# Cross attention by single key tiles in two score banks, maxima in the other two, running sums on GpSimd, attention output through DRAM

## The chip, the cores and the metric

The kernel runs on one core of a Trainium2 chip. The time is that of the device in microseconds, as the median of several runs; before the change it is 4902.3 us (three runs, 4899.26 to 4904.04).

## What is computed

A gated block on x of shape (8, 1024, 512) with a context of shape (8, 1024, 384), all in float32:

```python
x = x + tanh(g_xattn) * cross(layernorm(x), ctx)
x = x + tanh(g_ffn) * selfattn(layernorm(x))
# cross: 8 heads of 64; q = x Wq, k = ctx Wk, v = ctx Wv
#   softmax(q k^T / 8) v, then Wo and a bias
# selfattn: 16 heads of 32; q is normalized per head, shifted and scaled;
#   softmax(q k^T / sqrt(32)) v = h; a gate per token from softmax(h Wr) (best 3 of 15)
#   and softmax(h Ws); out = (h * gate) Wp + bias
```

Both attentions are full softmaxes over 1024 keys; the kernel subtracts a row maximum before each exponential.

## The kernel before

**Phases and chunks.** There are 16 phases: for each of the 8 batch elements one cross phase (kind 1) and one self phase (kind 2), in the order cross 0, cross 1, self 0, cross 2, self 1 and so on. A phase has four chunks of 128 channels, which are two heads of width 64 in a cross phase and four heads of width 32 in a self phase. A chunk goes through steps (`Chunk.steps`): for each half h of 512 queries, over the key tiles of 128. In a self phase a step is one key tile, so 16 steps a chunk; in a cross phase it is two key tiles (`nk` = 2), so 8 steps.

**A step.** `score` (line 677) multiplies k by q with the array cut into row groups of 32 or 64 ("rows" here), into two pairs of PSUM banks of the pool `ps_sc`, each pair one tile of 128 x 1024. At the first step of a half the negated row maxima (`sh`) are put in by a product with ones; later steps add the product with the difference of key tiles (`differences`, line 547), so the shift stays in the bank, and the scores of a step can be written only when the exponentials of the step before have been read. ScalarE takes the exponentials of each pair (line 723). `value` (line 824) multiplies them with v, with the array cut into column groups of 32 or 64 ("columns"), into one bank that is kept over a half. The sums of the exponentials: `paired` (line 728) adds two exponential tiles on GpSimd, `add` (line 735) adds such a result to the running one on VectorE if that is free and not `behind`, or else keeps it apart, and `summed` (line 756) multiplies what is left with ones on TensorE. A cross step pairs its own two tiles, a self step pairs with the next step. At the end of a half, ScalarE copies the values into `hT`, a tile in SBUF for each half, and `multiplied` (line 818) divides by the sum on GpSimd. `hT` has one buffer for each half, so a new phase may write it only when the output projection of the phase before has read it; `value` runs projections until that is so.

**Maxima.** For each coming chunk, all scores are computed once more beforehand in bfloat16 (`scores`, line 589) and reduced on VectorE. `unit` (line 600) does this for one head, 128 queries and 512 keys, in one of the three banks of `ps_gen`; a chunk has 32 (cross) or 64 (self) of them. `row_epoch` (line 913) puts some beside the scores of a step, `visit` (line 1010) does some between two column products, which changes the cutting of the array twice. When they are complete, `turn` transposes them and sends them to `sh` by DMA.

**Fills.** Between the steps lie the projections of other chunks and phases, the "fills", as two streams: `projector` (q and k of coming chunks) and `others` (output projection of the phase before, gates, and v of the next phase). They use the three banks of `ps_gen` too.

**What sets the order.** Each engine's order is fixed when the program is built. The builder keeps a clock for each engine (`clock`) with costs written by hand (`MM` 862 ns for a column product, `CHANGE` for a change of the array's cutting, `on("DVE", 690)` and so on), and decides by it. `attend` (line 958) goes through a chunk: scores of the next step, values of this one, then fills up to a quota from `COSTS`, and `until` waits, fills or visits until the scores' banks come free. `wanted` (line 975) gives the rate of maxima per step over three coming chunks, and `credit` adds it up.

Of the kernel before, what the change touches and what calls it, by code (L numbers as in the profile page):

```python
# [16 lines left out]
P = 128  # L17
# [4 lines left out]
def tile_gated_block(  # L22
# [62 lines left out]
    ps_sc = ctx.enter_context(tc.tile_pool(name="ps_sc", bufs=2, space=bass.MemoryType.PSUM))  # L85
# [106 lines left out]
    CHANGE = {(32, 128): 105, (64, 128): 105, (128, 32): 105, (128, 64): 110, (128, 128): 110}  # L192
    LOADED, LANDED, RATE = 3500, 5500, 0.0008
    COSTS = {1: (54, 28, 30, 30), 2: (50, 20, 22, 26)}
# [9 lines left out]
    deferred = []  # L204

# [77 lines left out]
    class Stream:  # L283

        def __init__(self, g):
            self.g = g
            self.step()
# [10 lines left out]
    def work(flow):  # L298

        ready = [(not s.mid, n) for n, s in enumerate(flow) if s.ready() <= now() + 20]  # L300
        if ready:
            s = flow[min(ready)[1]]
        else:
            s = min(flow, key=lambda s: s.ready())
            if s.ready() == NEVER:
                return False
        s.step()
        if not s.ready:
            flow.remove(s)
        flush()  # L310
        return True
# [101 lines left out]
    class Chunk:  # L413


        def __init__(self, kind, b, c):
# [4 lines left out]
            self.nk = 4 // self.nh  # L421
            self.ns = NT // self.nk
# [124 lines left out]
        def differences(self):  # L547

            w, n = self.nk * P, self.ns // 2
# [59 lines left out]

        def fours(self):  # L610
# [3 lines left out]
            for u in range(2):  # L614
# [13 lines left out]
            tiles = [  # L628
                ps_sc.tile([P, 2, H], F32, tag="sc", name=f"pm_{self.key}_{self.left}_{u}")
                for u in range(2)  # L630
            ]
# [45 lines left out]
        def score(self, step, order):  # L677
# [3 lines left out]
            if s == 0:  # L681
                self.pss = {}
                for u in order:
                    slot, free = least(places)
                    tile_u = ps_sc.tile([P, 2, H], F32, tag="sc", name=f"sc_{key}_{h}_{u}")
                    self.pss[u] = [tile_u, slot, free]
                    places[slot] = free

            def products(m, u):
                done = 0.0  # L690
                for j in (2 * u, 2 * u + 1):
                    kk, i = divmod(j, nh)
                    r, kc = i * width, s * self.nk + kk
# [5 lines left out]
                    else:  # L699
                        part = slice(r, r + width)  # L700
                        array((width, P))
                        lhsT, rhs = self.k[part, ts(kc, P)], self.q[part, ts(h, H)]
# [3 lines left out]
                        tile_u[:, j % 2, :],  # L706
# [9 lines left out]
            for half in [order] if self.kind == 1 else [order[:1], order[1:]]:  # L716
                for m in range(1 if s else 0, 2):
                    for u in half:
                        done[u] = products(m, u)
            e = {}  # L720
            for u in order:
                e[u] = Exps(f"e_{key}_{h}_{s}_{u}")
                nc.scalar.activation(e[u].tile, self.pss[u][0], AF.Exp)  # L723
                e[u].ready = on("ACT", 975, done[u], e[u].free)
                self.pss[u][2] = places[self.pss[u][1]] = e[u].ready
# [9 lines left out]
        def add(self, h, s, u, a, last):  # L735

            accs = self.acc.setdefault((h, u), [])
            wanted = not behind[0]
            free = clock["DVE"] <= now() + 500
            end = s + 1 >= self.ns  # L740
            if accs and not forced[0] and not (wanted and free) and not (end and now() > a.ready + 1500):
                later.insert(0, (now() + 200, self.add, h, s, u, a, last))
                return
            elif accs and wanted and (free or not end):
                nc.vector.tensor_tensor(accs[-1].tile, accs[-1].tile, a.tile, ALU.add)  # L745
                accs[-1].ready = on("DVE", 1820, accs[-1].ready, a.ready)
                a.used(accs[-1].ready)
                live[0] -= 1
                ready = accs[-1].ready
# [6 lines left out]
        def summed(self, h, end):  # L756

            accs = [self.acc.pop((h, u)) for u in range(self.nh // 2)]
# [59 lines left out]
        def multiplied(self, h, r, ready):  # L818
            hT = self.st.hT[h][:, self.c, :]
            engine = nc.vector if self.ends else nc.gpsimd  # L820
            engine.tensor_tensor(hT, hT, r, ALU.mult)  # L821
            self.st.hT_ready[h][self.c] = on("DVE" if self.ends else "POOL", 1270, ready)

        def value(self, step):

            h, s = step
            width, st = self.width, self.st
            if s == 0:
# [3 lines left out]
            for kk in range(self.nk):  # L832
                kc = s * self.nk + kk
                for i in range(self.nh):
                    j = kk * self.nh + i
                    nc.tensor.matmul(  # L836
                        self.av[ts(i, width), :],
                        lhsT=st.v[:, kc, ts(self.c * self.nh + i, width)],
                        rhs=e[j // 2].tile[:, j % 2, :],
                        start=(kc == 0),  # L840
                        stop=(kc == NT - 1),
                    )
                used = [e[kk]] if self.kind == 1 else [e[0], e[1]]
                done = pe(MM, av_free[0], *(x.ready for x in used))
                for x in used:
                    x.used(done)
                if kk == 0 and self.kind == 1:
                    room(1, self, h)
                    self.paired(h, s, 0, e[0], e[1], True)
                    array((P, width))  # L850
            if self.kind == 2 and s + 2 == self.ns and self.ends:
                for u in range(2):
                    self.whole[h, u] = [e[u], self.e[h, s + 1][u]]
                live[0] += 4
                later.append((now() + 3000, self.summed, h, True))
            elif self.kind == 2 and s % 2 == 0:
                room(2, self, h)
                for u in range(2):
                    self.paired(h, s + 1, u, e[u], self.e[h, s + 1][u], u == 1)
            if s == self.ns - 1:  # L860
                while st.before and st.before.hT_left[h]:
                    assert work(at_work)
                nc.scalar.copy(st.hT[h][:, self.c, :], self.av)
                av_free[0] = on("ACT", 590, done)
                self.divided(h, av_free[0])
            if s % 2 or self.kind == 1:
# [3 lines left out]
        def begun(self):  # L870
            self.whole = {}
            self.e, self.acc, self.parts, self.halves = {}, {}, {}, {}
# [23 lines left out]
    def room(n, ch, h):  # L896

        while live[0] > 5 - n:
# [14 lines left out]
    def row_epoch(ch, step, target, need, kept):  # L913
# [3 lines left out]
        order = (0, 1)  # L917
        at = now() + CHANGE.get(tiling[0], 0) + 30
        ok = target and target.pend and target.left and target.open <= at
        if ok and target.kind == 2 and ch.kind == 2:  # L920
            n = free_banks(at) - kept
# [4 lines left out]
            picks = [i for i in (2 * late, 2 * late + 1) if target.pend[i]]  # L926
            for i in picks[: max(n, 0)]:
                target.unit(i)
            order = (1 - late, late)
        elif ok and target.kind == 1 and free_banks(at) >= 2:  # L930
            for i in range(2):
                if target.pend[i]:
                    target.unit(i)
        ch.score(step, order)
        if not target or target.kind != ch.kind:
            return
        if ch.kind == 2:
            at = min(rows)
            if ok and target.left:
                n = max(free_banks(at + 30) - kept, 0)  # L940
                picks = [i for i in (2 * order[0], 2 * order[0] + 1) if target.pend[i]]
                for i in picks[:n]:
                    target.unit(i)
        elif need > 2 and target.left and target.open <= now() and free_banks(now()) - kept >= 2:
            for i in range(2):
                if target.pend[i]:
                    target.unit(i)

    at_work, at_side, debt = [], [], [0.0]
# [8 lines left out]
    def attend(ch, queue, first, cost):  # L958
# [3 lines left out]
        debt[0] = min(debt[0], 6 * MM) + cost * MM  # L962
        filled, owed = 0.0, debt[0]
        n = len(ch.steps)
        weight = 2 if ch.kind == 1 else 1
        after = queue[0] if queue else None
        credit, last = 0.0, now()

        def target():
            for t in queue[:3]:  # L970
# [4 lines left out]
        def wanted(m):  # L975

            slots, left, rate = (n - m) * weight - 4, 0, 0.0
            for t in queue[:3]:
                left += t.left if t.pend is not None else t.nh * NT * NH
                rate = max(rate, left / max(slots, 1))  # L980
                slots += len(t.steps) * (2 if t.kind == 1 else 1)
            return rate * weight
# [6 lines left out]
        def fill():  # L989
# [5 lines left out]
            debt[0] -= now() - was  # L995
# [14 lines left out]
        def visit(slack=300, least=2, keep=True):  # L1010
# [5 lines left out]
            n = free_banks(at) - (kept() if keep else 0)  # L1016
            some = sorted((i for i in range(t.nh) if t.pend[i]), key=lambda i: -len(t.pend[i]))
            if n < min(least, len(some)):
                return False
            for i in some[:n]:  # L1020
                t.unit(i)
                credit -= 1
            return True

        def until(at, urgent=False):
            while now() < at:
# [5 lines left out]
                if (urgent or credit >= 2) and visit():  # L1032
# [4 lines left out]
        def rows_of(chunk, step):  # L1037
            nonlocal credit
            t = target()
            if t and t.kind != chunk.kind and credit >= 2:  # L1040
                visit(600, keep=False)
            was = t.left if t else 0
            row_epoch(chunk, step, t, credit, 0)
            credit -= was - (t.left if t else 0)
# [5 lines left out]
        for m, step in enumerate(ch.steps):  # L1050
            need = wanted(m)
# [493 lines left out]
```

## Time and profile before

| | |
|---|---|
| profiled execution | 4899.77 us |
| its span, first to last instruction | 4897.9 us |
| clock granted to TensorE, mean | 0.983 |
| TensorE busy | 4792.1 us, 98% |
| VectorE busy | 2728.5 us, 56% |
| ScalarE busy | 2294.7 us, 47% |
| GpSimd busy | 2628.1 us, 54% |
| single maxima on VectorE (line 606) | 3042, mean 684 ns |
| pair adds on GpSimd (line 730) | 764, mean 2378 ns |
| running adds on VectorE (line 745) | 141, mean 1967 ns |
| matmuls of the sums (line 768) | 2524 |

How to read it: PE is TensorE's matmul, PEld its weight load, DVE VectorE, ACT ScalarE, POOL GpSimd and SP the queue of the DMAs. In a group's line the source line comes first, then engine, operation, out<-in by the program's names, shapes and count; behind the bar busy microseconds and the mean of one in ns, then the idle time of the engine just before them and who ended it. In a timeline a line begins with its start and its length. A product of float32 shows as two passes for each row or column group: the matmuls of one column product are 8 with groups of 32 and 4 with groups of 64. The first and the last matmul of such a group overlap, so times are best read from start to start.

### The profile page before, as it was taken

What the parts mean: (1) busy time and instruction counts of PE and PEld (TensorE: products, weight loads), DVE (VectorE), ACT (ScalarE), POOL (GpSimd) and SP (SyncE); (2) the same over time, 40 slices, a digit from 0 to 9 for tenths busy, and PEclk for the clock granted to TensorE, in tenths of its full rate; (3) what the DMA queues carried; (4) which work ended last, traced back from release to release, by engine and by line L of the source; (5) the groups of instructions that cost most, each with busy time, mean ns of one, the idle gap of its engine ahead of it and who ended that gap; (6) DMA issues with size and microseconds to landing.
All of it is one profiled execution on the core that took longest, in us unless ns stands there. A gap on an engine that the chain in (4) does not pass through costs nothing.

```text
span 4897.9 us, 76864 instructions
## 1 busy us (share of the span) xinstructions
PE 4792.1 (98%) x31628; PEld 1389.7 (28%) x31628; DVE 2728.5 (56%) x4377; ACT 2294.7 (47%) x3109; POOL 2628.1 (54%) x1474
## 2 busy tenths in 40 slices
PE   8999999999999999999999999999999999999998
PEld 2223222332222322233222332223322233222222
DVE  4676366554665536655366554665446554465564
ACT  4344355533554335543355433554335533355554
POOL 2455466544664446644566444664456634466564
PEclk9999999999999999999999999999999999999999
DMA  4012021210202102120021200212002020020000
GB/s 144 25 63 76 9 69 37 84 38 17 69 30 87 33 17 69 32 87 31 17 71 30 87 31 17 71 36 83 31 20 68 19 64 17 23 72 11 32 18 29
DMA packets 223153, 228.53 MB, mean 47 GB/s; under 512 B 24400, under 2 KB 147280, under 8 KB 222800
## 3 DMA queue, kind: packets, MB, share of 16 engines
q1 hardware_dynamic: 222512, 223.61, 14.4%
q8 instruction: 248, 4.06, 0.4%
q14 instruction: 105, 0.86, 0.1%
q10 hardware_dynamic: 288, 0.00, 0.0%
HBM read 158.13 MB, written 65.01 MB: 46 GB/s over the span
## 4 chain that ended last, share of the span: by engine, by line
PE 92%; DVE 5%; ACT 1%; DMA 1%; issue 1%; POOL 0%; SPq 0%; DVEq 0%; POOLq 0%; ACTq 0%
PE sc L705 20%; PE av L836 19%; PE pm L591 10%; PE pq L326 9%; PE po L326 9%; PE pk L326 8%; PE pv L326 8%; PE sum L768 7%; DVE mx L606 2%; PE pn L326 1%; DVE e L745 1%; ACT e L723 1%; PE pg L326 0%; DVE mv L344 0%; POOL e L730 0%
## 5 line engine op out<-in xcount | busy, mean ns | idle before, releaser
L606 DVE TENSOR_REDUCE mx<-pm 128x1 f32<-128x512 f32 x3042 | 1956.7, 684 | 1637.5 <-PE pm L591 1629.5
L730 POOL TENSOR_TENSOR e<-e,e 128x1024 f32<-128x1024 f32 x764 | 1805.7, 2378 | 1271.2 <-PE av L836 863.3
L723 ACT ACTIVATE e<-sc 128x1024 f32<-128x1024 f32 x1536 | 1488.2, 1020 | 944.5 <-PE sc L705 876.1
L705 PE MATMUL sc<-q,k 32*128 32x512 f32 (+1 forms) x6144 | 1173.3, 627 | 3.3 <-ACT e L723 3.3
L836 PE MATMUL av<-e,v 128*32 128x512 f32 (+1 forms) x6144 | 1063.0, 613 | 0.7 <-ACT e L723 0.7
L591 PE MATMUL pm<-kb,qb 32*128 32x512 bf16 (+1 forms) x3072 | 728.4, 388 | 66.0 <-DVE mx L606 53.1
L705 PEld LDWEIGHTS sc<-q,k 32*128 32x128 f32 (+1 forms) x6144 | 414.6, 187 | 321.0 <-issue 215.8
L591 PEld LDWEIGHTS <-qb 32*128 32x128 bf16 (+1 forms) x3072 | 171.8, 92 | 1133.3 <-issue 1101.4
L836 PEld LDWEIGHTS av<-e,v 128*32 128x32 f32 (+1 forms) x6144 | 207.1, 118 | 700.9 <-issue 659.4
L768 PE MATMUL sum<-e,ones 128*32 128x512 f32 (+1 forms) x2524 | 393.5, 611 | 9.8 <-DVE e L745 5.9
L745 DVE TENSOR_TENSOR e<-e,e 128x1024 f32<-128x1024 f32 x141 | 276.7, 1967 | 31.8 <-POOL e L730 30.9
L326 PE MATMUL pq<-y2T,wq 128*32 128x512 f32 (+1 forms) x1376 | 252.1, 601 | 0.0
L326 PE MATMUL pk<-y2T,wk 128*32 128x512 f32 (+1 forms) x1376 | 251.1, 601 | 0.0
L326 PE MATMUL pv<-wv,y2T 128*64 128x512 f32 (+1 forms) x1152 | 249.6, 601 | 0.0
L326 PE MATMUL pq<-y1T,wq 128*32 128x512 f32 (+1 forms) x1696 | 248.0, 597 | 1.2 <-ACT y1T L408 0.7
L326 PE MATMUL po<-wo,h1T 128*32 128x512 f32 (+1 forms) x1920 | 248.0, 598 | 0.0
L326 PE MATMUL po<-wo,h2T 128*64 128x512 f32 (+1 forms) x1280 | 231.2, 594 | 1.4 <-ACT rn L520 1.4
L326 PE MATMUL pk<-ctx,wk 128*32 128x512 f32 (+1 forms) x1272 | 189.9, 606 | 6.7 <-DMA ctx<-in_ctx 6.7
L768 PEld LDWEIGHTS sum<-e,ones 128*32 128x32 f32 (+1 forms) x2524 | 109.1, 120 | 275.3 <-issue 219.4
L326 PE MATMUL pv<-wv,ctx 128*32 128x512 f32 (+1 forms) x1440 | 182.2, 596 | 0.0
L821 POOL TENSOR_TENSOR h1T<-h1T,r 128x512 f32<-128x512 f32 x64 | 81.3, 1271 | 186.1 <-ACT r L806 117.5
L344 DVE SCALAR_TENSOR_TENSOR mv<-mv 128x1 f32<-128x1 f32 x128 | 95.2, 744 | 129.6 <-ACT mv L343 129.2
(114 smaller groups left out, 2818.4 us busy)
## 6 DMA issues: line engine op xcount, KB each, us to landing
y<-xn SPq DMA_DIRECT2D x120, 256.0 KB
xb<-y SPq DMA_DIRECT2D x480, 64.0 KB
x<-in_x SPq DMA_DIRECT2D x72, 256.0 KB
x1far<-x SPq DMA_DIRECT2D x64, 256.0 KB
x<-x1far SPq DMA_DIRECT2D x64, 256.0 KB
out<-x SPq DMA_DIRECT2D x64, 256.0 KB
xn<-in_x SPq DMA_DIRECT2D x56, 256.0 KB
ctx<-in_ctx SPq DMA_DIRECT2D x7, 1536.0 KB
```

The source lines that it names most:

```text
L326: nc.tensor.matmul(ps[ts(j, w), :], lhsT=lhsT[:, ts(j, w)], rhs=rhs, start=start, stop=stop)
L344: nc.vector.scalar_tensor_tensor(mv[..., 0:1], mv[..., 0:1], -1.0, mv[..., 1:2], ALU.mult, ALU.mult)
L591: nc.tensor.matmul(ps, lhsT=self.qb[ts(i, self.width), ts(c, P)], rhs=self.kb[ts(i, self.width), ts(kh, H)], start=True, stop=True,)
L606: nc.vector.tensor_reduce(self.mx[:, i * NT + c, kh : kh + 1], b.tile, AX.X, ALU.max)
L705: nc.tensor.matmul(tile_u[:, j % 2, :], lhsT=lhsT, rhs=rhs, start=(m == 0), stop=(m == 1), skip_group_check=True,)
L723: nc.scalar.activation(e[u].tile, self.pss[u][0], AF.Exp)
L730: nc.gpsimd.tensor_tensor(one.tile, one.tile, two.tile, ALU.add)
L745: nc.vector.tensor_tensor(accs[-1].tile, accs[-1].tile, a.tile, ALU.add)
L768: nc.tensor.matmul(b.tile[ts(2 * u + j, self.width), :], lhsT=ones[:, 0 : self.width], rhs=acc[n].tile[:, j, :], start=(n == 0), stop=(n = ...
L821: engine.tensor_tensor(hT, hT, r, ALU.mult)
L836: nc.tensor.matmul(self.av[ts(i, width), :], lhsT=st.v[:, kc, ts(self.c * self.nh + i, width)], rhs=e[j // 2].tile[:, j % 2, :], start=(kc ...
```

## The change

It does five things.

1. A cross step has one key tile, so 16 steps a chunk, and its scores use one pair of banks (`order = (0,)`). All four score banks become one PSUM tile `sc` of which `places` hands out halves.
2. In cross phases the other pair takes maxima: `two` computes those of two heads into it and reduces both in one instruction. `maxima` chooses between a pair and single banks, for the steps and the visits. `paired[0]` bars the pair in self phases and in the last steps before one.
3. One rate for maxima: `due` looks over six coming chunks, less 5 steps, and less 12 or 4 more for those behind the next. Visits between fills need a credit of 6, visits in a wait one of 4.
4. `add` takes GpSimd for the running sum if its clock is free (or within 2.5 us in a cross phase), or else VectorE, or keeps the tile apart.
5. The attention output goes to DRAM (`hfar`), 256 KB for each chunk and half, and `Reader` brings it back in tiles of 128 tokens, up to four ahead, for gates and output projections; the last chunk's last half is read from SBUF. Each stream of fills has an allowance of its own (`owed`, `spent`), the same for every chunk of a kind. Costs of leaving the column cutting in the builder's clock are 140 and 153 in place of 105 and 110.

```diff
-    COSTS = {1: (54, 28, 30, 30), 2: (50, 20, 22, 26)}
+    CHANGE = {(32, 128): 105, (64, 128): 105, (128, 32): 140, (128, 64): 153, (128, 128): 110}
+    LOADED, LANDED, RATE, LAG = 3500, 5500, 0.0008, 16 * 862
+    EARLY, LEAD, AFTER = 5, {1: 12, 2: 4}, 150
+    COSTS = {1: (18, 17), 2: (14, 15)}
...
+    sc = ps_sc.tile([P, 4, H], F32, tag="sc", name="sc")
...
-            self.nk = 4 // self.nh
-            self.ns = NT // self.nk
+            self.nu = self.nh // 2
+            self.ns = NT
...
+        def two(self, u):
+            self.begun_maxima()
+            c, kh = both = self.shared(u)[0]
+            slot, free = least(places)
+            held = sc[:, ts(slot, 2), :]
+            done = 0.0
+            for j in range(2):
+                i = 2 * u + j
+                self.pend[i].remove(both)
+                done = max(done, self.scores(held[:, j, :], i, c, kh, free))
+            out = self.mx.rearrange("p (i c) k -> p i c k", c=NT)[:, ts(u, 2), c, kh]
+            nc.vector.tensor_reduce(out, held, AX.X, ALU.max)
+            places[slot] = on("DVE", 1230, done)
+            self.taken(2)
...
         def add(self, h, s, u, a, last):
             accs = self.acc.setdefault((h, u), [])
             end = s + 1 >= self.ns
+            engine = None
+            if accs:
+                if clock["POOL"] <= now() + (2500 if self.kind == 1 else 0):
+                    engine = "POOL"
+                elif clock["DVE"] <= now() + 500 and not behind[0]:
+                    engine = "DVE"
+                elif not forced[0] and not (end and now() > a.ready + 1500):
+                    later.insert(0, (now() + 200, self.add, h, s, u, a, last))
+                    return
+                elif self.kind == 1 and clock["POOL"] <= now() + 4000:
+                    engine = "POOL"
+                elif not end and not behind[0]:
+                    engine = "DVE"
+            if engine:
+                on_it = nc.gpsimd if engine == "POOL" else nc.vector
+                on_it.tensor_tensor(accs[-1].tile, accs[-1].tile, a.tile, ALU.add)
...
         def multiplied(self, h, r, ready):
+            ph, hs = self.st, self.hs[h]
             engine = nc.vector if self.ends else nc.gpsimd
-            engine.tensor_tensor(hT, hT, r, ALU.mult)
+            engine.tensor_tensor(hs, hs, r, ALU.mult)
...
+                nc.sync.dma_start(out=ph.hfar[h][:, self.c, :], in_=hs)
+                ph.h_ready[h][self.c] = ready + LANDED
...
         def value(self, step):
+            while not st.v_done:
+                assert work(at_work)
...
-            elif self.kind == 2 and s % 2 == 0:
-                room(2, self, h)
+            elif s % 2 == 0:
+                room(self.nu, self, h)
...
-                while st.before and st.before.hT_left[h]:
-                    assert work(at_work)
...
+    def maxima(t, at, spare, pick=None, least_of=2):
+        n = free_banks(at) - spare
+        rows_left = [i for i in range(t.nh) if t.pend[i] and (pick is None or i in pick)]
+        pairs = []
+        for u in range(t.nu):
+            if {2 * u, 2 * u + 1} <= set(rows_left) and t.shared(u) and paired[0] and min(places) <= at:
+                pairs = [u]
...
+        rows_left = [i for i in rows_left if i // 2 not in pairs]
...
+        for u in pairs:
+            t.two(u)
+        for i in rows_left:
+            t.unit(i)
+        return 2 * len(pairs) + len(rows_left)
...
+        def due(m):
+            rate, units = 0.0, 0
+            for k, t in enumerate(queue[:6]):
+                units += t.left if t.pend is not None else t.nh * NT * NH
+                rate = max(rate, units / max(n - m + n * k - EARLY - (LEAD[ch.kind] if k else 0), 1))
+            return rate
...
+            rate = due(m)
+            credit = min(credit + rate, 8)
+            behind[0] = rate > 4
+            paired[0] = ch.kind == 1 and not (after and after.kind == 2 and m > n - 4)
...
-            if credit >= 3:
-                visit()
             quota = owed * (m + 1) / n
             while flow and filled < quota and ready() <= now() + 20:
-                if credit >= 2:
+                if credit >= 6:
                     visit()
...
+    class Reader:
...
+                n = len(self.tiles)
+                h = n // NQ
+                nk = ND - 1 if self.last and h == 1 else ND
+                if n >= self.used + 4 or max(ph.h_ready[h][0:nk]) > now():
+                    return NEVER
+                ht = work_pool.tile([P, ND, P], F32, tag="ht", name=f"ht_{ph.key}_{n}", bufs=4)
+                nc.sync.dma_start(out=ht[:, 0:nk, :], in_=ph.hfar[h][:, 0:nk, ts(n % NQ, P)])
+                self.tiles[n], self.ready[n] = ht, now() + LOADED
...
+            at_work[:] = [s for s in chains if s.ready]
+            for s, cost in zip(chains, COSTS[ph.kind]):
+                s.owed = max(min(s.owed, s.spent + 6 * MM), s.spent - 8 * MM) + cost * MM
```

## The prediction

> **What bounds the kernel now.** I read the page's shares first, then its chain, then one steady pair of phases (a cross phase at 1531.7 to 1822.5 us, the self phase behind it to 2139.2), by windows, by groups and by the timeline of PE.
>
> ```profile
> PE 4792.1 (98%) x31628; PEld 1389.7 (28%) x31628; DVE 2728.5 (56%) x4377; ACT 2294.7 (47%) x3109; POOL 2628.1 (54%) x1474
> ...
> PE 92%; DVE 5%; ACT 1%; DMA 1%; issue 1%; POOL 0%; SPq 0%; DVEq 0%; POOLq 0%; ACTq 0%
> PE sc L705 20%; PE av L836 19%; PE pm L591 10%; PE pq L326 9%; PE po L326 9%; PE pk L326 8%; PE pv L326 8%; PE sum L768 7%; DVE mx L606 2%; PE pn L326 1%; DVE e L745 1%; ACT e L723 1%; PE pg L326 0%; DVE mv L344 0%; POOL e L730 0%
> ```
>
> PE is the end of the chain nearly everywhere. So time goes only if PE gets fewer matmuls, fewer changes of its tiling, or fewer holes. Of its rows, the maxima (pm, 10%) and the sums of exponentials (sum, 7%) can shrink without changing what is multiplied.
>
> ```profile
> 1531.70:1822.50 290.80, 289.49 (x1446) 90.06 (x1448) 141.87 (x246) 107.67 (x146) 124.35 (x75) 0.99 0.14 44
> 1822.50:2139.20 316.70, 309.95 (x2461) 83.08 (x2453) 192.26 (x299) 177.48 (x241) 203.78 (x109) 0.98 0.16 51
> ```
>
> The columns are length, then busy PE, PEld, DVE, ACT, POOL. A pair of phases takes 607.5 us, and in the self phase POOL is idle for 316.7 - 203.8 = 113 us, in the cross phase for 166.
>
> ```profile
> 1159.67 1.99 PE L705 MATMUL sc<-q,k 64*128 64x512 f32 x8
> 1161.59 1.94 PE L836 MATMUL av<-e,v 128*64 128x512 f32 x8
> 1163.46 0.39 PE L591 MATMUL pm<-kb,qb 32*128 32x512 bf16 x2
> 1163.78 1.94 PE L326 MATMUL pk<-y2T,wk 128*64 128x512 f32 x8
> ...
> 1391.89 1.90 PE L768 MATMUL sum<-e,ones 128*32 128x512 f32 x16
> 1393.61 1.90 PE L326 MATMUL pq<-y1T,wq 128*32 128x512 f32 x16
> ```
>
> Read start to start, these give every price. Two column products without a change between: 1393.61 - 1391.89 = 1.72, so one **slot** is 0.86. Scores of two key tiles are two slots, but take 1161.59 - 1159.67 = 1.92: 0.20 over. Then two slots of values take 1.87: 0.15 over for leaving and entering the column tiling. So a **turn** to rows that carries scores costs 0.35 beyond its slots. A turn with maxima alone costs 0.32 + 0.15 = 0.47. From the first matmul of a turn to the first one behind it, medians over the whole timeline of PE: scores of two key tiles alone 1.92, with a pair of maxima of the same width in front 2.04, behind 2.13, with a pair of the other width in front 2.24. So such a pair costs 0.12, 0.21 or 0.32, wherever it rides along.
>
> Counted in the same timeline, a cross phase has 32 turns with scores and 40 with maxima alone, a self phase 64 and 38.
>
> **Part by part, per pair of phases.**
>
> *Single key tiles.* A cross phase has 64 steps of one key tile in place of 32 of two. Slots of scores and values stay. 32 more turns x 0.35 = **+11.2**. Nearly every turn now has its pair of maxima in front; before, of 42 pairs about half lay behind the scores: 21 x 0.09 = -1.9. Net **+9.3**; I see no gain in this edit by itself. The page TensorEngine Tiling of the Trainium skill (Key Properties) says that changing the tiling mode drains TensorE; it gives no time for it. By that rule alone the change could only lose, and the trace gives that loss its size.
>
> *Maxima in the other score pair.* The 64 turns with scores take 2 cross maxima each without a bank of the fills: 128 places against the 84 single maxima that went into such turns before, so 22 turns of two fall away. The 64 maxima of the next self chunk can go four at a time (a score pair and two banks) in front of scores, 16 more turns. That is 38 of 78 turns with maxima alone; bounds 0 (the rate still asks for as many visits: it counts six chunks ahead, wants 12 steps of lead in a cross phase, and visits at a credit of 6) and 60. I take 32: 32 x 0.47 = **-15.0**. Those put in front of scores of the other width cost 0.32 each, as above: 12 more of them, **+3.8**. On DVE a pair takes one reduction (the group of line 637: 1216 ns) in place of 2 x 684; DVE is at 142 of 291, so this is worth nothing directly.
>
> *Sums.* The groups of the two windows:
>
> ```profile
> L768 PE MATMUL sum<-e,ones 128*64 128x512 f32 x72 | 16.6, 592 | 0.0
> ...
> L768 PE MATMUL sum<-e,ones 128*32 128x512 f32 x232 | 30.9, 629 | 0.7 <-DVE mx L606 0.7
> ...
> L730 POOL TENSOR_TENSOR e<-e,e 128x1024 f32<-128x1024 f32 x31 | 73.4, 2368 | 76.1 <-PE av L836 74.8 <-issue 1.4
> ...
> L730 POOL TENSOR_TENSOR e<-e,e 128x1024 f32<-128x1024 f32 x65 | 153.4, 2381 | 82.1 <-ACT e L723 40.0 <-PE av L836 38.1 <-PE pm L591 4.0
> ```
>
> 72 / 4 = 18 slots in the cross phase; 232 / 8 and 16 / 4 of the other width, 33, in the self phase. With everything added before, each would need 8 (four chunks, two halves). `add` (line 735) now gives the running add to POOL. In the cross phase it may wait up to 2.5 us for POOL and POOL has 166 us: 24 adds x 2.37 = 57 fit, so 18 becomes 9: **-7.7**. In the self phase one slot less costs two adds; all 24 slots would take 48 x 2.38 = 114, all that is idle, and `add` takes POOL only when it is free. I take half: 12 slots, 24 adds, **-10.3**; bounds 0 and 24 slots (-20.6). What gets late next: the pair adds of line 730 queue behind, and with them the free exponential buffers; at 204 + 57 = 261 of 300 there is room.
>
> A rule against this part: GPSIMD Engine Reference of the Trainium skill (4.1, Engine selection) puts elementwise adds on VectorE and calls GpSimd about 2x slower for two inputs. Here line 730 takes 2.38 and line 745 on DVE a median of 1.23 alone but up to 3.40 (mean 1967 ns over 141). The rule prices the add and not what waits for it: no PE row above waits for POOL. By the rule the adds would stay on DVE and the sums' gain would be none.
>
> *Attention output through DRAM, allowances, one rate.* No PE work is added. Per pair of phases 16 writes and 16 reads of 256 KB more, on an SP queue whose DMAs are 14.4% of the engines' time; 67 MB on top of 224 makes about 19%. The writes wait on SP for the multiply on POOL; behind them are weights, rows and the shift rows of line 668, for which PE waited 2.6 us in all. The nearest wait is that of SP for POOL in front of the x1 writes: 50 times, 210.6 us, longest 9.8. The reads are asked for four tiles ahead, beside 2 slots of fill a step; if that cover goes, one wait of 6.2 a phase (SP's longest for a read behind an x1 write) is +12.4 a pair. The other side: output projections are no longer forced ahead of the first values, and DVE adds less, so holes may close. I added up intervals between PE starts that no change explains: 15.3 us for the pair at 1200 to 1800, 146 in the whole kernel, and who ends them is DVE:
>
> ```profile
> PE pm L591 <- DVE mx L606: 53.1, 115, 8.7
> PE sc L705 <- ACT e L723: 3.3, 4, 1.2
> ```
>
> Bounds -12 and +12; I take **-3**, near the rows of today, since five steps of earliness aim at the boundary holes but a queue is added. The loop from scores to exponential to next scores is now one pair deep: 0.23 + 0.86 + about 0.3 to the exponential + 1.02, some 2.4, against 1.18 + 0.15 + 0.86 = 2.2 of PE's own; any fill hides the 0.2, and there are over 2 slots a step.
>
> **Sum** per pair: 9.3 - 15.0 + 3.8 - 7.7 - 10.3 - 3 = -22.9; eight pairs (I take the first and last phases for as good as the steady ones) give -183. The profiled execution took 4899.77 us (span 4897.9, 1.9 around it), so 4717; the median of the three runs lies 2.5 higher, so on that footing about **4719**.
>
> **Rivals.**
> - *The sums fall but not the turns*: the rate spends what the score pair saves on more maxima ahead. 9.3 + 3.8 - 18.0 = -4.9, with 3 of holes -8 a pair: 4838. For it: 4 maxima a step are wanted in self phases and three banks still serve them. Against: the 128 places.
> - *The change doesn't do what it says*: POOL is never found free in self phases, turns as before: 9.3 - 7.7 = +1.6, with the 3 of holes -1.4, so 4915 or 4891, and about 4902 between.
> - *POOL becomes the bound* (slower). Place: self phases. If 48 adds go there, POOL has 204 + 114 = 318 us of work; a sixth of the 82 us that it now waits in front of line 730 remains, 332 against 316.7: +15 a pair. The cross phase gives back 5 (9.3 + 3.8 - 7.7, and 21 of the turns saved, -9.9): +10 x 8 = 4982. It decides once load and waits pass the some 302 us to which PE shrinks, (302 - 204 - 14) / 2.38, at 35 adds. For it: exponential buffers are nine and the order on every engine is fixed beforehand. Against: the condition on POOL's clock in `add`.
>
> **Chances.** Forecast 0.53 (own range 4650 to 4790), sums alone 0.19, no change 0.05, POOL bound 0.18, and 0.05 for more than the forecast's range (60 turns and 20 slots: 4600). Faster 0.77, same 0.05, slower 0.18, with 0.2% (10 us) as what a measurement can tell. The range 4640 to 4930 leaves out most of the slow case and the best one.
>
> **What would show it.** Sum rows: 2524 matmuls now; about 2524 - 8 x (36 + 96) = 1470 if right. Maxima-only turns: 46 a pair; scores of width 64 in twice the turns. POOL busy 75% or less; over 90% is the slow case. Waits of PE for DMA of ht, or of ACT's e for POOL, would make me wrong.

## The result, and the profile after

The changed kernel takes 5613.64 us (median of four runs, 5606.63 to 5617.69) against 4901.24 for the kernel before, also of four runs: a ratio of 1.145, 95% interval 1.143 to 1.147. It is 712 us slower, where the prediction had it 183 us faster. The profiled execution has a span of 5615.8 us at a mean granted clock of 0.973.

First the page of the changed kernel: the shares, then the chain of work that ended last, by engine and by line.

```profile
PE 4796.2 (85%) x30804; PEld 1323.9 (24%) x30804; DVE 2621.3 (47%) x3759; ACT 2323.0 (41%) x3099; POOL 3215.9 (57%) x1712
...
PE 72%; DVE 13%; ACT 6%; POOL 4%; issue 2%; DMA 2%; SPq 0%; DVEq 0%; ACTq 0%; POOLq 0%
PE sc L727 18%; PE av L873 13%; DVE mx L633 9%; PE pq L334 8%; PE pv L334 7%; PE pk L334 7%; PE po L334 7%; ACT e L744 5%; PE sum L800 4%; PE pm L599 4%; PE sc L599 3%; POOL e L753 2%; POOL e L777 1%; DVE mx L614 1%; PE pn L334 1%
```

TensorE is as long busy as before (4796 against 4792 us) with 824 fewer matmuls, but in a span that is 718 us longer. It has lost its place as the end of the chain nearly everywhere: 92% became 72%, and VectorE rose from 5% to 13%, 9% of it on one line, 633, the reduction of a pair of maxima. No engine is full, so time went into waits. The waits of PE (total, times, longest):

```profile
PE sc L727 <- DVE mx L633: 576.9, 414, 3.3
PE sc L727 <- ACT e L744: 80.1, 87, 3.3
PE pm L599 <- DVE mx L614: 30.1, 58, 5.0
```

The scores (line 727) waited 414 times, 1.39 us each on average, for a reduction of maxima. It is that of the pairs, of which there are 553:

```profile
L633 DVE TENSOR_REDUCE mx<-sc 128x2 f32<-128x1024 f32 x553 | 677.4, 1225 | 1523.7 <-PE sc L599 801.9 <-PE pm L599 686.5 <-ACT hs L894 35.3
```

Nothing in the arithmetic asks for that wait: the maxima of line 633 belong to a chunk still to come. A timeline of the changed kernel (start, length, then the idle time before in brackets) shows the same step with and without a pair:

```profile
279.63 1.23 DVE L633 TENSOR_REDUCE mx<-sc 128x2 f32<-128x1024 f32 x1 [1.67 <-PE sc L599]
...
280.91 1.13 PE L727 MATMUL sc<-q,k 64*128 64x512 f32 x4 [1.39 <-DVE mx L633]
...
281.97 1.08 PE L873 MATMUL av<-e,v 128*64 128x512 f32 x4
...
282.98 0.39 PE L599 MATMUL pm<-kb,qb 64*128 64x512 bf16 x2
...
283.21 1.13 PE L727 MATMUL sc<-q,k 64*128 64x512 f32 x4
283.40 1.29 DVE L614 TENSOR_REDUCE mx<-pm 128x1 f32<-128x512 f32 x2 [2.55 <-PE pm L599]
...
285.46 0.39 PE L599 MATMUL sc<-kb,qb 64*128 64x512 bf16 x2
...
285.96 1.23 DVE L633 TENSOR_REDUCE mx<-sc 128x2 f32<-128x1024 f32 x1 [1.27 <-PE sc L599]
287.24 0.39 PE L727 MATMUL sc<-sh,ones_b 1*128 1x512 bf16 x2 [1.38 <-DVE mx L633]
```

The scores at 280.91 begin 0.05 us after the reduction that started at 279.63 has ended. The next pair shows the whole row: maxima into `sc` at 285.46, their reduction until 287.19, and only at 287.24 the first product of the next scores. At 283.21 the maxima in front went to the single banks of `pm`; the scores follow them at once and VectorE reduces beside them. What tells the two apart is the tile: `sc` is one tile of four banks, the pair lies in one half and the scores go to the other, and the scores wait for a reader of the half that they do not touch.

### The profile page after: what moved, and what is told of

Its sections match the earlier page's. It is cut to its first block, busy times and chain, and to the rows that moved or that the text cites. A ratio compares the mean times of both kernels' runs of the same rounds, so it can differ in the third digit from the quotient of the medians.

```text
span 5615.8 us, 76017 instructions
## 1 busy us (share of the span) xinstructions
PE 4796.2 (85%) x30804; PEld 1323.9 (24%) x30804; DVE 2621.3 (47%) x3759; ACT 2323.0 (41%) x3099; POOL 3215.9 (57%) x1712
## 4 chain that ended last, share of the span: by engine, by line
PE 72%; DVE 13%; ACT 6%; POOL 4%; issue 2%; DMA 2%; SPq 0%; DVEq 0%; ACTq 0%; POOLq 0%
PE sc L727 18%; PE av L873 13%; DVE mx L633 9%; PE pq L334 8%; PE pv L334 7%; PE pk L334 7%; PE po L334 7%; ACT e L744 5%; PE sum L800 4%; PE pm L599 4%; PE sc L599 3%; POOL e L753 2%; POOL e L777 1%; DVE mx L614 1%; PE pn L334 1%
## 5 line engine op out<-in xcount | busy, mean ns | idle before, releaser
L753 POOL TENSOR_TENSOR e<-e,e 128x1024 f32<-128x1024 f32 x764 | 1819.2, 2396 | 1447.4 <-ACT e L744 1352.4
L614 DVE TENSOR_REDUCE mx<-pm 128x1 f32<-128x512 f32 x1936 | 1249.5, 684 | 791.9 <-PE pm L599 786.0
L633 DVE TENSOR_REDUCE mx<-sc 128x2 f32<-128x1024 f32 x553 | 677.4, 1225 | 1523.7 <-PE sc L599 801.9
L873 PE MATMUL av<-e,v 128*32 128x512 f32 (+1 forms) x6144 | 1135.9, 627 | 0.0
L777 POOL TENSOR_TENSOR e<-e,e 128x1024 f32<-128x1024 f32 x238 | 565.8, 2377 | 7.4
L599 PE MATMUL pm<-kb,qb 32*128 32x512 bf16 (+1 forms) x1942 | 471.7, 387 | 40.9 <-DVE mx L614 30.1
L334 PE MATMUL po<-wo,ht 128*32 128x512 f32 (+1 forms) x3072 | 497.2, 605 | 4.7 <-DVE mx L614 4.2
L853 POOL TENSOR_TENSOR hs<-hs,r 128x512 f32<-128x512 f32 x126 | 166.1, 1318 | 408.2 <-ACT hs L894 257.8
L800 PE MATMUL sum<-e,ones 128*32 128x512 f32 (+1 forms) x1792 | 276.0, 598 | 8.1 <-DVE mx L614 6.1
L599 PE MATMUL sc<-kb,qb 64*128 64x512 bf16 (+1 forms) x1130 | 224.4, 393 | 40.9 <-DVE mx L661 10.7
L777 DVE TENSOR_TENSOR e<-e,e 128x1024 f32<-128x1024 f32 x86 | 208.6, 2439 | 33.5 <-POOL e L753 32.9
```

Of the source, the lines that this page charges most:

```text
L334: nc.tensor.matmul(ps[ts(j, w), :], lhsT=lhsT[:, ts(j, w)], rhs=rhs, start=start, stop=stop)
L599: nc.tensor.matmul(ps, lhsT=self.qb[ts(i, self.width), ts(c, P)], rhs=self.kb[ts(i, self.width), ts(kh, H)], start=True, stop=True,)
L614: nc.vector.tensor_reduce(self.mx[:, i * NT + c, kh : kh + 1], b.tile, AX.X, ALU.max)
L633: nc.vector.tensor_reduce(out, held, AX.X, ALU.max)
L753: nc.gpsimd.tensor_tensor(one.tile, one.tile, two.tile, ALU.add)
L777: on_it.tensor_tensor(accs[-1].tile, accs[-1].tile, a.tile, ALU.add)
```

## Theories and experiments

**Theory A**: the halves of the one tile `sc` wait for each other in the program, so a reduction between a pair's matmuls and the scores is put on TensorE's path. **Theory B**: the loop from scores to exponential to the next scores, now one pair deep, is the new limit, and the wait for VectorE only stands in front of it. **Theory C**: the way of the attention output through DRAM, with its queue, is the new limit.

**Two tiles in place of one** in the changed kernel; the order of the instructions is the same on every engine.

```diff
-    sc = ps_sc.tile([P, 4, H], F32, tag="sc", name="sc")
+    sc = [ps_sc.tile([P, 2, H], F32, tag=f"sc{n}", name=f"sc{n}") for n in range(2)]
...
-            held = sc[:, ts(slot, 2), :]
+            held = sc[slot]
```

> The changed kernel with its four score banks as two PSUM tiles of two banks in place of one tile of four; nothing else. Theory A (halves of one tile wait for each other: scores that write one half wait until VectorE has read the other): of the 945 us that I add up between matmul starts beyond what a change of tiling explains, about 800 go, as many as the kernel before does not have: 4815 us, at least under 4950, and the wait of the scores' matmul for the reduction of maxima (577 us in 414 waits) falls under 30 us. Theory B (the loop from scores to exponential to next scores is too long with one pair): the wait only changes its name to the exponential, and the time stays over 5400. Theory C (the DRAM path of the attention output and its queue): over 5400 too.

4869.51 us; 0.994 of before (0.992 to 0.995). One declaration is worth 744 us, more than the whole loss. The page and a timeline of this version:

```profile
PE 4704.9 (97%) x30804; PEld 1316.5 (27%) x30804; DVE 2640.0 (54%) x3759; ACT 2322.7 (48%) x3099; POOL 3222.2 (66%) x1712
```

```profile
269.61 0.39 PE L599 MATMUL sc<-kb,qb 64*128 64x512 bf16 x2
...
269.86 1.13 PE L727 MATMUL sc<-q,k 64*128 64x512 f32 x4
...
270.05 1.23 DVE L633 TENSOR_REDUCE mx<-sc 128x2 f32<-128x1024 f32 x1 [0.97 <-PE sc L599]
...
270.91 1.08 PE L873 MATMUL av<-e,v 128*64 128x512 f32 x4
```

The reduction now runs beside the scores, and the turn takes 270.91 - 269.61 = 1.30 us. Over the whole timeline a turn with scores of one key tile and a pair of the same width in front has a median of 1.18 us here and of 2.84 in the changed kernel. Of the scores' waits, 576.9 us for the reduction and 80.1 for the exponential, this is left:

```profile
PE sc L727 <- ACT e L744: 18.4, 23, 2.3
...
PE sc L727 <- DVE mx L633: 2.5, 6, 0.4
```

The Trainium skill says in PSUM — Partial Sum Buffer (PSUM bank collisions raise a hardware error) that accesses are to be guarded by bank and quadrant. The two halves are different banks, so by that rule too the wait was not needed, and the rows above show scores and reduction side by side. Theory A holds: the order on every engine is the same and GpSimd, the loop and the way through DRAM are as they were.

**One tile in the kernel before**, its halves handed out in turn:

```diff
+    sc = ps_sc.tile([P, 4, H], F32, tag="sc", name="sc")
...
-                    tile_u = ps_sc.tile([P, 2, H], F32, tag="sc", name=f"sc_{key}_{h}_{u}")
+                    tile_u = sc_half()
```

> The kernel before with its two score tiles as halves of one tile of four banks, handed out in the same turn; nothing else. Theory A: each half's scores now wait for the exponential of the other half as well. That exponential is the second of the two and 1.02 us later; values and about two slots of fills (2.6 us) lie between, so most of it is hidden: 1 to 4% slower, 4950 to 5100. Theories B and C: no part of theirs is in it, no change.

4927.94 us; 1.005 of before (1.004 to 1.007): slower, as expected, but by 25 us and so less than the 1 to 4% expected. The wait of PE that grew is

```profile
PE sc L712 <- ACT e L730: 35.4, 55, 1.7
```

against 3.3 us, 4 times, before. In this run only 12 reductions work in `sc`, all of them before 75 us, so only exponentials are waited for, and mostly they are done by then. One tile alone is not the price; a foreign reader between two writers of it is.

**No pairs**, in the changed kernel and then with two tiles:

```diff
-            paired[0] = ch.kind == 1 and not (after and after.kind == 2 and m > n - 4)
+            paired[0] = False
```

> The changed kernel, one tile of four banks and single key tiles kept, with no maxima in the free score pair (all of them in single banks). Theory A: nothing else writes or reads the tile during a cross phase, so the wait of scores for the pair's reduction goes; more turns for maxima alone and VectorE at 684 ns each come back: 4850 to 5050. Theory B: the single pair's loop is still there: over 5400. Theory C: over 5400.

> The two-tile version with all maxima in single banks, none in the free score pair. By the prediction the pairs are worth 32 turns of 0.47 less 3.8 a pair of phases, 90 us: 4960. By the measured 4869 with pairs and 5039 for one tile without pairs, 60 to 170 us slower than with pairs, less what the one tile costs in self phases (its waits for exponentials, 86 us): about 4950. If single key tiles alone were no loss, under 4900.

5039.18 us (1.028 of before, 1.027 to 1.030) with one tile and 5018.83 (1.025, 1.023 to 1.026) with two. The first lies in its range, the second is 69 us above the 4950 expected. Without pairs the tile matters 20 us, with them 744: the loss needs both parts together. And with two tiles the pairs are what they were meant to be, and worth more than the 90 us of the prediction: 5018.8 - 4869.5 = 149 us gained.

**The running adds.** Four kernels take GpSimd's adds away or put them in alone. On VectorE only, as the rule before, in the version with two tiles:

```diff
-                if clock["POOL"] <= now() + (2500 if self.kind == 1 else 0):
-                    engine = "POOL"
...
+                if wanted and (free or not end):
+                    engine = "DVE"
```

> The two-tile version, with the running sums of exponentials added on VectorE alone by the old rule in place of GpSimd first. If the sums' step of the prediction holds, sums come back as matmuls: 1792 now to some 2300 or more, (2300 - 1792) / 8 to / 4 is 64 to 127 slots of 0.86, so 55 to 110 us slower than the two-tile version. If adds on GpSimd delay the exponential buffers by as much as they save, no difference.

4933.95 us (1.007 of before, 1.005 to 1.008): all of GpSimd's adds together are worth 64 us. The builder decides by its clocks, so here and in the next runs the order of other work moves too. Then in the kernel before, in self phases only and in cross phases only, both without the 2.5 us that a cross phase of the changed kernel may wait for GpSimd:

```diff
+                if self.kind == 2 and clock["POOL"] <= now():
+                    engine = "POOL"
```

> The kernel before with the new rule for the running sums in self phases alone (GpSimd when its clock is free, then VectorE); all else as before. By the prediction's step, some 10 to 12 slots of 0.86 a self phase go: 70 to 80 us faster, 4825. By what the two-tile versions with and without GpSimd's adds showed (64 us for both kinds of phase): 30 to 45 us faster. If GpSimd then delays its pair adds: no gain or slower.

```diff
+                if self.kind == 1 and clock["POOL"] <= now():
+                    engine = "POOL"
```

> The kernel before with the new rule for the running sums in cross phases alone; all else as before. By the prediction's step 9 slots of 0.86 a cross phase go: 62 us faster, 4840. By the measured worth of both together, 20 to 35 us faster.

Self phases alone: 4979.59 us (1.017, 1.015 to 1.018), 81 us slower where a gain was expected. Cross phases alone: 4865.28 us (0.993, 0.992 to 0.995), 34 us faster, as expected. So there the adds in self phases cost more than the sum matmuls that they save. Without them in the version with two tiles:

```diff
-                if clock["POOL"] <= now() + (2500 if self.kind == 1 else 0):
+                if self.kind == 1 and clock["POOL"] <= now() + 2500:
```

> The changed kernel with two score tiles, and with GpSimd's running adds only in cross phases; in self phases the running adds are VectorE's or are kept apart, as before. Theory G (the running adds on GpSimd in self phases bring more holes than the sum matmuls that they take away, as they did when put into the kernel before by themselves, +81 us): below 4866, about 4790 to 4840, with holes back towards 150 us. Rival H (the effects add up: without any running adds on GpSimd this kernel took 4934, with all of them 4869, and those of the cross phases alone brought the kernel before 34 us, so those of self phases bring about 31 here): about 4890 to 4910. In both the sum slots lie between 256 and 408.

4833.65 us (0.986, 0.985 to 0.988): 36 us better than with them, though TensorE has 200 sum matmuls more. The waits of ScalarE point at how they cost. In the kernel before with adds in self phases, and then in the changed kernel with two tiles:

```profile
ACT e L723 <- POOL e L752: 88.6, 46, 3.9
```

```profile
ACT e L744 <- POOL e L777: 49.0, 27, 5.7
```

An exponential may not be written until GpSimd's add has read the tile that was in its buffer; later scores wait for the exponential. One buffer more, with the same order of instructions, tests that in the version with two tiles and in the one with adds in cross phases only (where the builder's own list of buffers has ten too):

```diff
-    epool = ctx.enter_context(tc.tile_pool(name="epool", bufs=9))
+    epool = ctx.enter_context(tc.tile_pool(name="epool", bufs=10))
```

> The changed kernel with two score tiles and all of GpSimd's running adds, with ten buffers for the exponentials in place of nine; the order of the instructions is the same on every engine. Theory W (the running adds on GpSimd in self phases cost by holding buffers: the exponentials waited 49 us, 27 times, for the running adds on GpSimd, and the scores behind them): these waits go, and the time falls by 15 to 40 us to about 4830 to 4850. Rival X (the adds cost otherwise, by what else queues behind them on GpSimd, or by sharing memory with VectorE): within 5 us of 4866.

> The version with GpSimd's running adds only in cross phases, with ten buffers for the exponentials; the order of the instructions is the same on every engine. There the exponentials waited only 3 us for GpSimd's adds and 14 for VectorE's, so by theory W a gain of 0 to 12 us: 4822 to 4834. By X nothing: 4834.

With all of GpSimd's adds, 4843.95 us (0.989, 0.987 to 0.990), 26 less than with nine buffers, and the wait shrinks:

```profile
ACT e L744 <- POOL e L777: 10.6, 7, 3.2
```

With adds in cross phases only, 4831.05 us (0.986, 0.985 to 0.988), 3 less than with nine and not told apart from it. The kernel before was 4 us faster in this series, so the tenth buffer brings 22 to 26 of the 36 us; what makes the rest is open. In the kernel before, where the same adds cost 81 us, no run had a tenth buffer: that the cost there has the same cause is likely by the 88.6 us of waits, but not shown.

**The writes to DRAM.** The builder issues the write of `hs` on SP before the multiply on GpSimd is due, and SP stands at it for 1499 us in all in the version with two tiles. Issued only when it is due by the builder's clock:

```diff
-                nc.sync.dma_start(out=ph.hfar[h][:, self.c, :], in_=hs)
+                Later(ready, self.sent, h, hs, ready)
```

> The two-tile version, with the writes of the attention output to DRAM issued when GpSimd's multiply should be done by the builder's clock, in place of at once. In the two-tile version SP stands 1499 us in 122 waits for that multiply, and PE has holes that end with a DMA behind it (weights 25 us, shift rows 14). If the queue is what makes those holes: 30 to 40 us faster than the two-tile version, about 4835. If the holes come from elsewhere: within 10 us of it.

4866.72 us (0.994, 0.992 to 0.995), the time of the version with two tiles. But the edit hardly did what it was for: SP still stands at that multiply for 1481.3 us in 116 waits, against 1499.0 in 122. So the run doesn't tell whether the queue makes the holes that end with a DMA.

**Single key tiles, nearly alone**: two tiles, no pairs, adds on VectorE (both edits above together). The output through DRAM, the allowances and the one rate remain.

> The changed kernel with two score tiles, no maxima in the score pair, and the running adds on VectorE as before: what is left of the change is single key tiles, the output through DRAM, the allowances and the one rate. The prediction's terms give 11.2 - 3 a pair of phases for these, 66 us, so about 4967. If pairs are worth 149 us here too, as with GpSimd's adds, it is 4934 + 149 = 5083, and then 180 us, not 66, are the price of these parts alone. About 5020 if the pairs are worth the 90 us that they were first thought to be.

5132.11 us (1.047, 1.045 to 1.049): 230 us slower than before, over three times the 66 of the prediction's terms. So without pairs these parts are a heavy loss, and pairs are worth 198 us in this company (5132 - 4934). The spans differ by 225 us. Added up as in the table below, 17 of them are turns with scores, 118 turns with maxima alone, 51 the sums (457 slots against 397.5, as VectorE made only 79 running adds where it had made 141), and about 39 are left in the column stretches.

## Why the prediction was wrong

The step that failed is the price of a pair: "such a pair costs 0.12, 0.21 or 0.32, wherever it rides along", and with it the wait for its reduction on VectorE, which has no term in the sum. Those prices were measured on maxima in banks that share no tile with scores. The change put the pair into the tile of the scores, and 414 times the reduction stood on TensorE's path with 1.39 us. With two tiles the price holds: 1.18 us with a pair of the same width in front, 1.06 without, a difference of 0.12. The bounds of 12 us a pair of phases for holes covered neither the 72 us that came (577 / 8) nor any mechanism for it. The edit was in the diff and in the description ("all four score banks become one PSUM tile"); the prediction costed what is multiplied and reduced, and gave that line no price at all. What it named as a possible new wait, the loop one pair deep, is small: of the 80 us that the scores waited for line 744 the two tiles leave 18. The slower rival, GpSimd as the bound, did not happen either: GpSimd is busy 57%. But its argument, nine exponential buffers and an order fixed beforehand, came true in part (22 to 26 us), and so did a sign that the prediction had named, waits of ACT's `e` for POOL: 50.1 us, 27 times, in the changed kernel.

The other steps can be judged in the version with two tiles, where the order is that of the changed kernel. I added up the timeline of PE from start to start, against the kernel before; the predicted terms are times eight. A turn to rows is what lies from its first matmul to the next column product, and each turn more or less adds 0.15 for the way back. Holes inside a turn are in the rows of the turns and in that of the holes, so that the sum meets the spans to 2 us is partly luck; the column stretches alone are 75 us longer than sums and ways back explain.

| step | predicted | with two tiles | how |
|---|---|---|---|
| turns with scores | +105 | +90 | 1400.6 to 1451.7 us; 257 turns more x 0.15 |
| turns with maxima alone | -120 | -71 | 611 to 406 turns, 235.8 to 195.5 us; 205 x 0.15 less |
| sums | -144 | -122 | 397.5 to 256 slots x 0.86 |
| holes | -24 | +72 | 146 to 218 us |
| sum | -183 | -31 | spans: 4869.3 - 4897.9 = -29 |

- *Single key tiles and merges*: near in sum. But the experiment with single tiles nearly alone shows that the price depends on pairs: 577 maxima found room in its 512 turns with cross scores, where 606 had it in 255 turns before, the self scores carried 1015 in place of 1206, and turns with maxima alone rose from 611 to 704. "I see no gain in this edit by itself" was right and too kind.
- *Maxima in the other score pair*: 205 turns of 611 went, not 256: the cross scores carried 1187 maxima in place of 606, but the self scores only 997 in place of 1206, which the prediction did not count. Those left have a mean of 0.48 us in place of 0.39. The usual turn of two is as long as before, a median of 0.32 in both; the mean is raised by one stretch of 32 matmuls at 80.3 us, which takes 21.6, and by some turns that hold waits. Direction right, size six tenths.
- *Sums*: the groups of the changed kernel show the step itself nearly as forecast, 1792 matmuls against the 1470 that were to show it:

```profile
L777 POOL TENSOR_TENSOR e<-e,e 128x1024 f32<-128x1024 f32 x238 | 565.8, 2377 | 7.4
...
L800 PE MATMUL sum<-e,ones 128*32 128x512 f32 (+1 forms) x1792 | 276.0, 598 | 8.1 <-DVE mx L614 6.1
```

  Each add takes 2.38 us, as priced, and there are 238 where 48 a pair of phases, 384, were counted. What failed is "there is room": GpSimd had room on average, but in self phases not at the moment when a buffer was needed. So GpSimd's adds gained 64 us, not 144; in self phases they cost. The rule that elementwise adds belong on VectorE (GPSIMD Engine Reference of the Trainium skill, 4.1), which the prediction set aside because no PE row waited for GpSimd, would have been right for the self phases and wrong for the cross phases.
- *Output through DRAM, allowances, one rate*: not told apart from each other here. What the queue of the writes costs is open, since the run that was to ease it left SP's wait nearly whole.

With one declaration mended and the adds in self phases left to VectorE the idea is faster than the kernel before, 4833.65 us, a gain of 1.4%; the predicted 183 us were not reached by any version.

## What to carry to other kernels

When an edit joins buffers into one tile, price every reader of one half as a wait of every writer of the other, and look what order the program gives them: here the joined tile cost 20 to 25 us until a reduction stood between its writers, and then 744. A price from the trace holds for the buffers that it was measured in. And room on an engine by busy time says nothing on whether it is free at the right moment: an add that holds one of a few buffers used in turn for 2.4 us more has to be set against the next use of that buffer.

## What was not expected of the hardware

TensorE's clock can fall without a long hole. Windows of the changed kernel (length, then busy PE, PEld, DVE, ACT, POOL, then the granted clock):

```profile
284.00:288.00 4.00, 2.50 (x12) 0.86 (x12) 1.92 (x3) 1.02 (x1) 2.46 (x2) 1.00 0.00 0
288.00:290.00 2.00, 2.00 (x8) 0.29 (x4) 0.00 (x0) 0.81 (x1) 2.00 (x1) 0.52 0.00 0
290.00:294.00 4.00, 2.61 (x10) 0.41 (x6) 2.30 (x2) 0.80 (x2) 0.19 (x1) 0.81 0.00 0
```

After four microseconds in which PE was busy for 2.50, the clock is 0.52, and the value products of 289.07 take 1.97 us in place of 1.08. Between 270 and 288 us TensorE had four waits of 1.38 or 1.39 us and none that was longer. Most of the 414 waits were not followed by such a fall: by the clocks of the last two windows it cost an estimated 1.7 us, and 414 of that would be 700, far above the 152 that the clock took in all (below). What sets it off was not tested. But in all, waits cost more than their own length: the stretches of column products, which have the same matmuls in both, took 3288 us in the changed kernel and 3208 with two tiles. An estimate from the mean clocks: (1 - 0.973) x 5616 = 152 against (1 - 0.980) x 4869 = 97 us lost to the clock, so up to 54 of these 80. TensorE: Matmul & The Clock Gate of the Trainium skill (Part 1) gives an idle window of about 3.4 us as what lowers the clock; here the longest wait of the scores was 3.3 us, and those before this fall were of 1.4.
